# Layer 0 of a four-layer network: products as column tiles, a norm without broadcast rows, whole attention steps, the last gates in two streams on chip

## The chip, the cores and the metric

The kernel runs as one program on one NeuronCore of a Trainium2 chip. Its engines have queues of their own and run side by side: TensorE (PE in the profile, with its weight loads, PEld), VectorE (DVE), ScalarE (ACT), GpSimd (POOL) and SyncE (SP), which here issues most DMAs. The metric is the device time of one execution in microseconds. Before the change three timed runs gave 4085.17, 4080.33 and 4074.14, so a median of 4080.33 us. All data are float32, and a float32 product of this kernel appears in the trace as two records, each of them a weight load and a matmul.

## The reference, cut to layer 0

The network takes x (8 images, 256 channels, 32 x 32) through a convolution and attention layer, a deformable convolution, an attention and feed-forward layer, and an attention and expert layer. The change lies in the first of these:

```python
def _ln(x, w, b):
    r = lax.rsqrt(jnp.mean(x * x, axis=1, keepdims=True) + LN_EPS)
    return x * r * w[:, None, None] + b[:, None, None]

def _attention(x, ...):
    qkv = _bn(_conv1x1(x, qkv_w), ...).reshape(B, NH, 2 * KD + HD, N)
    q, k, v = (qkv[:, :, :KD], qkv[:, :, KD:2 * KD], qkv[:, :, 2 * KD:])
    attn = jax.nn.softmax(jnp.einsum('bhkn,bhkm->bhnm', q, k) * SCALE, axis=-1)
    out = jnp.einsum('bhdm,bhnm->bhdn', v, attn).reshape(B, Cc, H, W)
    pe = _bn(_dwconv3(v_img, pe_w), ...)
    return _bn(_conv1x1(out + pe, proj_w), ...)

def _edffn(x, pi_w, dw_w, fft_p, po_w):
    x = _dwconv3(_conv1x1(x, pi_w), dw_w)
    x1, x2 = (x[:, :hid], x[:, hid:])
    x = _conv1x1(jax.nn.gelu(x1, approximate=False) * x2, po_w)
    ...
    xp = jnp.fft.irfft2(jnp.fft.rfft2(xp) * fft_p, s=(PS, PS))
    ...

def _forward(x, ...):
    x = x + gamma1 * _attention(_ln(x, norm1_w, norm1_b), ...)
    return x + gamma2 * _edffn(_ln(x, norm2_w, norm2_b), ...)
```

Here NH is 4 heads, KD 32, HD 64, N = 1024 positions, the hidden width is 512 (so `pi_w` makes 1024 channels), and the FFT works on patches of 8 x 8.

## The kernel before

`fast0` is layer 0. Channels lie on partitions: an image is a tile of 128 partitions x 2 x 1024 (KC = 2 halves of the channels, N positions, worked on in halves of HF = 512[...]).

**Streams.** Each piece of the work is a Python generator that yields between pieces: `attention()` runs over all batches; `before_attention(b)`, `before_gates(b)`, `gates(b)` and `transforms(b)` each treat one batch. `by_time` merges them: every stream has a start and a step, and the one with the smallest due time is asked for its next piece. Time is counted in yields of the attention, two to a step, so 32 to a batch (T). A compiler pass may move instructions between engines' queues by their dependences afterwards, except those that are pinned[...].

**One attention step** (16 to a batch: two halves of the queries `gq`, eight blocks of keys `kt`) makes the scores `s` of four heads (L1442, four row tiles of 32 x 128 side by side) into two of the PSUM tiles `S`, the exponentials `e` (L1448, ACT), and, after a yield, `values(i - 1)`: the sums of the exponentials on DVE (L1398, L1402) and the products with the values into `A` (L1406, column tiles of 128 x 32). After the eighth block `finish` copies `A` to `av`, sums over keys by a product `D` (L1421), inverts it by Ln and Exp (L1425, L1426), multiplies and adds on DVE (L1428, L1429), makes `proj` (L78) and adds the input (`x`, loaded at L1393, two buffers), and stores to `mid` in DRAM.

**Norm** (`normed`, L1263 to L1285): squares on ACT; the mean over channels as products `ms` in two column tiles of 64, one for each half of the positions (L1272); Ln and Exp to `r`; two products with a row of ones, `rb` (L1281), spread each row over all partitions; ACT copies them from PSUM (L1284); DVE multiplies (L1285).

**Before attention**: norm, `qkv` (L78 through `linear`), the values transposed (`vT`, L1348), and the 3 x 3 depthwise term `pe` by products on three shifted copies (`thrice`, loaded from DRAM at L1361, one buffer).

**Gates**: eight chunks of 128 channels. For each, `pi` (L78) goes through a bank to `hp` (L1487), then a depthwise 3 x 3 convolution to `a`: the middle tap on ACT (L1289), eight taps on DVE (L1296). In the last batch chunks 1 and 7 go through `by_products` instead: 18 products with diagonal matrices `dg` (L1304, L1311). Chunks 0 to 3 pass a gelu (L1512, between two table loads), chunks 4 to 7 multiply them (`gate`, L1501), and the result is stored to `gated` in DRAM (L1502).

**Transforms**: for each of four pairs of patch columns `pr`, `hc` comes back from `gated` (L1526), then `po` (L1540), `fwd` (L1548), a multiply by `gain` (L1550), `back` (L1555), each with an ACT copy out of PSUM, and the residual add (`xc`, L1562) and store (L1563).

All of `qkv`, `proj`, `pi`, `po`, `fwd`, `back`, `ms`, `rb`, `D`, `vT`, `pe` share the two PSUM banks of `bank` (tag X) while attention runs, and four after it. When `attention()` ends, its pools are closed and the rest is merged with `net.head()`, which starts the weights and the first batch of layer 1 (`fast1`). Layer 1's own steps (`row`, `ax`, `ay`, `wt`, and the products `acc`) come after layer 0's last piece in program order, and take space that layer 0 gives up.

`columns` (L1023) and `linear_columns` (L1028) exist already and are used in layer 3; they write one product as four of 32 columns each:

```python
    def columns(self, ps, lhsT, rhs, **flags):
        for h in range(P // 32):
            self.nc.tensor.matmul(ps[32 * h : 32 * h + 32], lhsT=lhsT[:, 32 * h : 32 * h + 32], rhs=rhs, **flags)
```

Of the kernel before, what the change touches and what calls it, by code (L numbers as in the profile page):

```python
# [1156 lines left out]
def fast0(net, io):  # L1157
# [5 lines left out]
    BY_PRODUCTS, HROWS = (1, 7), IMG // 2  # L1163
    yield HOLD
    with ExitStack() as ctx, ExitStack() as att:
# [97 lines left out]
        def normed(xn, x, sq):  # L1263

            squares = [sq(k) for k in range(KC)]
            for k in range(KC):
                nc.scalar.activation(squares[k], x[:, k, :], AF.Square)
            yield
            ps = bank("ms")
            for k in range(KC):  # L1270
                for h in range(2):
                    nc.tensor.matmul(  # L1272
                        ps[64 * h : 64 * h + 64], lhsT=net.mean64, rhs=squares[k][:, bass.ts(h, HF)],
                        start=(k == 0), stop=(k == KC - 1),
                    )
            r = one.tile([P, HF], F32, tag="r", name="r")
            net.rsqrt(r, ps, net.eps6)
            yield
            for h in range(2):
                pr = bank("rb")  # L1280
                nc.tensor.matmul(  # L1281
                    pr, lhsT=net.unit[64 * h : 64 * h + 1, :], rhs=r[64 * h : 64 * h + 1, :], start=True, stop=True
                )
                nc.scalar.copy(squares[0][:, bass.ts(h, HF)], pr)  # L1284
            nc.vector.tensor_tensor(xn, x, squares[0].unsqueeze(1).to_broadcast([P, KC, N]), ALU.mult)  # L1285
# [33 lines left out]
        def before_attention(b):  # L1319
# [6 lines left out]
            def projected(d, w, j, norm):  # L1326
                for h in range(2):
                    ps = bank("qkv")
                    net.linear(ps, w, xn, bass.ts(j, P), bass.ts(h, HF))
                    nc.scalar.activation(d[:, bass.ts(h, HF)], ps, AF.Identity, scale=sc(norm), bias=sh(norm))  # L1330
# [11 lines left out]
            for t4 in range(0, NT, 4):  # L1342
                for t2 in (t4, t4 + 2):
                    ps = bank("vT")
                    for i in range(2):
                        for c in range(KC):
                            lo = i * C + c * P
                            nc.tensor.transpose(ps[:, lo : lo + P], v[:, c, bass.ts(t2 + i, P)], net.ident)  # L1348
                    nc.scalar.copy(va[:, t2 : t2 + 2].rearrange("p t c d -> p (t c d)"), ps)
                yield  # L1350
# [31 lines left out]
        def attention():  # L1382
# [4 lines left out]
            def values(i):  # L1387
                b, gq, kt = steps[i]
                e = es.pop(i)
                first, last = kt == 0, kt == NT - 1  # L1390
                if first:
                    state["x"] = atwo.tile([P, KC, HF], F32, tag="x", name="x")
                    nc.sync.dma_start(out=state["x"], in_=io.src[b][:, :, bass.ts(gq, HF)])  # L1393
                    state["A"] = psA.tile([P, KC, HF], F32, tag="A", name="A")
                elif kt == 1:
                    state["sum"] = aone.tile([P, NH, HF], F32, tag="sum", name="sum")
                    for j in range(2):
                        nc.vector.tensor_tensor(state["sum"][:, 2 * j : 2 * j + 2], state["e"][j], e[j], ALU.add)  # L1398
                else:
                    for j in range(2):  # L1400
                        half = state["sum"][:, 2 * j : 2 * j + 2]
                        nc.vector.tensor_tensor(half, half, e[j], ALU.add)  # L1402
                state["e"] = e
                for c in range(KC):
                    for h in range(NH):
                        nc.tensor.matmul(  # L1406
                            state["A"][32 * h : 32 * h + 32, c, :], lhsT=vas[b][:, kt, c, 32 * h : 32 * h + 32],
                            rhs=e[h // 2][:, h % 2, :], start=first, stop=last,
                        )
                if last:  # L1410
                    later.append(finish(b, gq, state["A"], state["sum"], state["x"]))
                    next(later[0])

            def finish(b, gq, A, total, x):
# [17 lines left out]
                for c in range(KC):  # L1432
                    ps = bank("proj")
                    net.linear(ps, wproj, o, bass.ts(c, P), cols)
                    nc.scalar.activation(av[:, c], ps, AF.Identity, bias=sh(6 + c))
# [3 lines left out]
            for i, (b, gq, kt) in enumerate(steps):  # L1439
# [9 lines left out]
                yield  # L1449
                later = [f for f in later if next(f, f) is None]  # L1450
                if i:
                    values(i - 1)
                yield
            values(len(steps) - 1)
            for f in later:
                for _ in f:
                    yield

# [9 lines left out]
        def before_gates(b):  # L1468
            xn = xs[b] = one.tile([P, KC, N], F32, tag="xn2", name="xn2")
            nc.sync.dma_start(out=xn, in_=mids[b])  # L1470
            yield

            def square(k):
                return five.tile([P, N], F32, tag="a", name="sq") if k else one.tile([P, N], F32, tag="sq", name="sq")

            yield from normed(xn, xn, square)
            yield

        def gates(b):
            xn = xs.pop(b)  # L1480

            def convolved(i):
                hp = two.tile([P, N], F32, tag="hp", name="hp")
                for h in range(2):
                    ps = bank("pi")
                    net.linear(ps, wpi, xn, bass.ts(i, P), bass.ts(h, HF))
                    nc.scalar.activation(hp[:, bass.ts(h, HF)], ps, AF.Identity, bias=pib[:, i : i + 1])  # L1487
                a = cv[i] = five.tile([P, N], F32, tag="a", name="a")
                yield
                if b == B - 1 and i in BY_PRODUCTS:  # L1490
                    yield from by_products(a, hp, i)
                else:
                    yield from depthwise(img(a), img(hp), lambda t_: dw_taps[:, i, t_ : t_ + 1])

            cv, sts = {}, {}

            def gate(j):
# [4 lines left out]
                nc.sync.dma_start(out=gated[b][:, j], in_=sts.pop(j))  # L1502

            for j in (0, 2):
# [3 lines left out]
                for i in (j, j + 1):  # L1508
                    sts[i] = two.tile([P, 4, 2, P], F32, tag="st", name="st")
                    a = cv.pop(i)  # L1510
                    for pc in range(2):
                        net.pinned(nc.scalar.activation(paired(sts[i], pc), patches(a, pc), AF.Gelu))  # L1512
                net.pinned(nc.scalar.preload_act_table_set("natural_log_exp_and_others"))
                yield
                gate(j)
                yield from convolved(5 + j)
# [3 lines left out]
        def transforms(b):  # L1520
# [12 lines left out]
            for pr in range(4):  # L1533
# [4 lines left out]
                for pc in range(2):  # L1538
                    for k in range(4):
                        nc.tensor.matmul(  # L1540
                            ps[:, bass.ts(pc, C)], lhsT=hc[:, k, pc, :], rhs=wpo[:, k, :],
                            start=(k == 0), stop=(k == 3),
                        )
# [3 lines left out]
                ps = bank("fwd")  # L1547
                nc.tensor.matmul(ps, lhsT=fwd, rhs=u.rearrange("p t c -> p (t c)"), start=True, stop=True)  # L1548
                nc.scalar.copy(u.rearrange("p t c -> p (t c)"), ps)  # L1549
                nc.vector.tensor_tensor(u, u, gain.unsqueeze(1).to_broadcast([P, 2, C]), ALU.mult)  # L1550
                yield
                back = bank("back")
                for c in range(KC):
                    for pc in range(2):
                        nc.tensor.matmul(  # L1555
                            back[:, (2 * c + pc) * P : (2 * c + pc + 1) * P], lhsT=u[:, pc, bass.ts(c, P)],
                            rhs=inv, start=True, stop=True,
                        )
                nc.scalar.copy(u.rearrange("p t c -> p (t c)"), back)
                for c in range(KC):  # L1560
                    xt = x[:, c, :].rearrange("p (h q w) -> p q h w", q=2, w=16)
                    nc.vector.tensor_tensor(xt, u[:, c].rearrange("p (q h w) -> p q h w", q=2, w=16), xt, ALU.add)  # L1562
                nc.sync.dma_start(out=io.dst[b][:, :, bass.ts(pr, C)], in_=x)  # L1563
                yield


        T = 32
        main = attention()
        streams = [(0, 1, main)]
        for b in range(B):  # L1570
            streams += [
                (T * (b - 1) - 2, 32 / 21, before_attention(b)) if b > 1 else (11 * b, 1.0, before_attention(b)),
                (T * (b + 1) + 7.4, 0.9, before_gates(b)),
                (T * (b + 1) + 10.5, 32 / 44, gates(b)),
                (T * (b + 2) + 11.5, 2, transforms(b)),
            ]
        for _ in range(10):
# [3 lines left out]
        own["X"], own["diag"] = io.pool(ctx, "f0t", 4, PSUM), io.pool(ctx, "f0d", 2)  # L1581
        by_time(rest + [[T * B + 1, 2, net.head()]])

# [1780 lines left out]
```

## Time and profile before

| | |
|---|---|
| timed runs, median (lowest to highest) | 4080.33 us (4074.14 to 4085.17) |
| the profiled execution: its time, its span | 4139.9 us, 4138.1 us |
| mean granted TensorE clock | 0.949 |
| busy, share of the span: PE, PEld, DVE, ACT, POOL | 91%, 43%, 61%, 55%, 14% |
| layer 0's exponentials L1448 | 256, from 52.5 to 1191.7 us |
| layer 0's last residual add (L1562) | 1407.66 us |
| layer 1's first product into `acc` (L1737) | 1412.05 us |

The profile is that of one execution. A row of the groups names a line, an engine, an operation with its output and inputs, the shape and the number of records, then the busy time in us and the mean length of one in ns, then the idle time of the engine before them and what ended it. Records of matmuls overlap, and their ends are modelled, so the time between two starts tells more than a length. A row of the timeline has the start in us, the time it covers, the engine and line, and in brackets the idle time before it and what ended that. Some matmul records are missing from the trace.

### The profile page before, as it was taken

To read this page: it belongs to the slowest core of one execution; us is meant where nothing else is said; L and a number is where in the kernel's file an instruction comes from. 1 tells how busy PE (TensorE), PEld (TensorE's weight loads), DVE (VectorE), ACT (ScalarE), POOL (GpSimd) and SP (SyncE) were. 2 spreads that over 40 slices of the span, in tenths; PEclk is the share of its full clock that TensorE was granted. 3 is DMA by queue.
4 is the path that set the end of the run, shared out by engine and by line. 5 is a ranking of instruction groups with operands and counts; after the bars stand their busy time and mean duration, and the time that the engine had idled before them with its cause. 6 is when DMAs were issued, how large, how long until landed. Compare 5 with 4: busy or idle time off the path is not lost. (4 is left out here: it accounts for less than half of the span.)

```text
span 4138.1 us, 59047 instructions
## 1 busy us (share of the span) xinstructions
PE 3755.4 (91%) x22502; PEld 1791.9 (43%) x22502; DVE 2522.3 (61%) x5030; ACT 2296.6 (55%) x3122; POOL 571.5 (14%) x646
## 2 busy tenths in 40 slices
PE   8999999999978787889999969899999999998997
PEld 3323333333334444454444525663333333326886
DVE  2398798798896489942232255753365666567345
ACT  4556656556553377734334345535776666675554
POOL 0000000000000000000000012431000150044653
PEclk9999999999888898989999979999999999999998
DMA  3313223223121578720000012432320141055666
GB/s 101 114 44 112 100 69 122 94 72 116 64 98 52 175 257 291 266 84 21 21 21 21 31 51 95 132 122 76 108 97 27 39 141 39 22 160 185 204 214 220
DMA packets 209974, 442.64 MB, mean 107 GB/s; under 512 B 22025, under 2 KB 132572, under 8 KB 197140
## 3 DMA queue, kind: packets, MB, share of 16 engines
q1 hardware_dynamic: 186580, 387.21, 28.4%
q0 software_dynamic: 19440, 46.45, 3.4%
q10 hardware_dynamic: 3664, 5.11, 0.4%
q8 instruction: 181, 2.97, 0.3%
q14 instruction: 109, 0.89, 0.1%
HBM read 283.34 MB, written 162.28 MB: 108 GB/s over the span
## 5 line engine op out<-in xcount | busy, mean ns | idle before, releaser
L1296 DVE SCALAR_TENSOR_TENSOR a<-hp,w_f_vec,a 128x961 f32<-128x961 f32 (+1 forms) x496 | 609.1, 1234 | 105.3 <-ACT a L1289 96.6
L2763 ACT ACTIVATE e<-s,five 128x1024 f32<-128x1024 f32 x512 | 542.8, 1112 | 218.1 <-PE s L2757 207.9
L2757 PE MATMUL s<-q,k 32*128 32x512 f32 x2048 | 312.4, 641 | 0.7 <-issue 0.5
L2737 PE MATMUL A<-e,v 128*32 128x512 f32 x2048 | 275.5, 610 | 17.7 <-DVE o L2742 16.0
L1448 ACT ACTIVATE e<-s 128x1024 f32<-128x1024 f32 x256 | 250.3, 1024 | 71.6 <-PE s L1442 60.9
L1402 DVE TENSOR_TENSOR sum<-sum,e 128x1024 f32<-128x1024 f32 x192 | 230.7, 1221 | 86.5 <-ACT e L1448 86.5
L1406 PE MATMUL A<-e,va 128*32 128x512 f32 x2048 | 265.6, 618 | 0.0
L2445 DVE SCALAR_TENSOR_TENSOR junk<-mo_x,w_f_wr 128x256 f32<-128x256 f32 x512 | 250.0, 488 | 13.5
L78 PE MATMUL pi<-xn,w_l_wpi 128*128 128x512 f32 x512 | 244.4, 619 | 14.2 <-ACT u L1549 9.2
L1442 PE MATMUL s<-q,k 32*128 32x512 f32 x1024 | 180.8, 648 | 2.5 <-ACT e L1448 2.5
L2964 PE MATMUL h<-xk,w 128*128 128x128 f32 x1192 | 155.6, 283 | 22.0 <-DVE xk L2950 14.8
L1058 POOL DMA_INDIRECT res<-y,to x149 | 150.5, 1010 | 134.4 <-DVE y L2988 75.6
L1753 PE MATMUL acc<-wt,z 128*64 128x192 f32 (+4 forms) x1344 | 130.0, 337 | 39.8 <-DVE wt L1808 39.2
L2757 PEld LDWEIGHTS s<-q,k 32*128 32x128 f32 x2048 | 93.3, 183 | 167.8 <-issue 160.9
L2964 PEld LDWEIGHTS h<-xk,w 128*128 128x128 f32 x1192 | 150.9, 198 | 29.2 <-DVE xk L2950 15.8
L78 PEld LDWEIGHTS pi<-xn,w_l_wpi 128*128 128x128 f32 x512 | 95.2, 196 | 152.4 <-issue 114.2
L2933 ACT COPY w<-w_l3f_w 128x512 f32 x149 | 92.1, 629 | 123.5 <-PE h L2964 82.8
L1058 POOL DMA_INDIRECT so<-xl,rows x128 | 130.4, 1019 | 172.1 <-issue 146.9
L1487 ACT ACTIVATE hp<-pi,pib 128x512 f32<-128x512 f32 x128 | 87.3, 691 | 120.2 <-PE pi L78 120.2
L2984 PE MATMUL y<-w_l3f_w,hid 128*128 x596 | 147.1, 389 | 3.8 <-issue 1.6
L1357 POOL MEMSET thrice<- 32x128 f32 x32 | 6.3, 197 | 1012.7 <-PE pe L1373 1012.7
L2258 PE MATMUL y<-w_l2f_w,hid 128*128 128x256 f32 x512 | 126.5, 402 | 17.4 <-issue 17.2
(412 smaller groups left out, 6959.0 us busy)
## 6 DMA issues: line engine op xcount, KB each, us to landing
row<-shifts SPq DMA_DIRECT2D x144, 512.0 KB
x<-d SPq DMA_DIRECT2D x31, 1024.0 KB
xs<-so SPq DMA_DIRECT2D x73, 260.0 KB
so<-zero SPq DMA_DIRECT2D x5, 3380.0 KB
thrice<-vimg SPq DMA_DIRECT2D x64, 256.0 KB
gated<-st SPq DMA_DIRECT2D x32, 512.0 KB
hc<-gated SPq DMA_DIRECT2D x32, 512.0 KB
xl<-mox SPq DMA_DIRECT2D x64, 256.0 KB
```

What stands on the lines that cost most here:

```text
L78: self.nc.tensor.matmul(ps, lhsT=w[:, i, m], rhs=src[:, i, cols], start=(i == 0), stop=(i == k - 1))
L1058: made = self.nc.gpsimd.indirect_dma_start(**args)
L1296: nc.vector.scalar_tensor_tensor(to, fr, taps(t_), to, ALU.mult, ALU.add)
L1402: nc.vector.tensor_tensor(half, half, e[j], ALU.add)
L1406: nc.tensor.matmul(state["A"][32 * h : 32 * h + 32, c, :], lhsT=vas[b][:, kt, c, 32 * h : 32 * h + 32], rhs=e[h // 2][:, h % 2, :], start= ...
L1442: nc.tensor.matmul(ss[h // 2][:, h % 2], lhsT=ks[b][32 * h : 32 * h + 32, bass.ts(kt, P)], rhs=qs[b][32 * h : 32 * h + 32, bass.ts(gq, HF) ...
L1448: nc.scalar.activation(es[i][j], ss[j], AF.Exp, scale=SCALE)
L2445: nc.vector.scalar_tensor_tensor(junk, xn[:, t, :], 1.0, self.wr[:, e, :], ALU.mult, ALU.mult, accum_out=pr[:, t, e : e + 1])
L2737: nc.tensor.matmul(A[32 * h : 32 * h + 32], lhsT=vs[b][:, kt, c * P + 32 * h : c * P + 32 * h + 32], rhs=e[:, h, :], start=first, stop=last,)
L2757: nc.tensor.matmul(ss[h // 2][:, h % 2], lhsT=ks[b][32 * h : 32 * h + 32, c, bass.ts(kt, P)], rhs=qs[b][32 * h : 32 * h + 32, c, bass.ts(h ...
L2763: anchor[:] = [nc.scalar.activation(e[:, 2 * j : 2 * j + 2], ss[j], AF.Square, scale=SCALE, bias=five)]
L2964: nc.tensor.matmul(ps[:, j, m], lhsT=ws[j][:, k, bass.ts(m, P)], rhs=xk[:, j, k], start=(k == 0), stop=(k == KC - 1),)
```

## The change

1. `qkv`, `proj`, `pi`, `po`, `fwd` and `back` are written as four column tiles of 32.
2. The norm makes the mean in four column tiles of 32 for each half of the positions, so that all 128 partitions hold it; Ln takes it from PSUM, one Exp follows; `r`, `rb` and the copies are gone. Both squares of the second norm are taken from the tag `a`, and `xn2` has two buffers.
3. An attention step is one piece instead of two: scores and exponentials, `values(i - 1)`, one piece of each waiting `finish`, yield. T is 16, and the starts and steps of the streams are given anew. `x` has one buffer and is loaded at `kt == 4`.
4. `vT` yields after each bank; `before_gates` has one yield more; `gate(j)` comes after the first piece of the next chunk.
5. The last batch: chunks 1 and 5 go by products; `begun` runs chunks in two streams in turn; the gated tiles stay on chip (`kept`), its transforms are in `gates`, with the first three chunks of `po` for all four `pr` ahead of the last gate, into four banks; `hp` has four buffers there (`late`), `diag` one.

```diff
-            ps = bank("ms")
-            for k in range(KC):
-                for h in range(2):
-                    nc.tensor.matmul(
-                        ps[64 * h : 64 * h + 64], lhsT=net.mean64, rhs=squares[k][:, bass.ts(h, HF)],
-                        start=(k == 0), stop=(k == KC - 1),
-                    )
-            r = one.tile([P, HF], F32, tag="r", name="r")
-            net.rsqrt(r, ps, net.eps6)
-            yield
             for h in range(2):
-                pr = bank("rb")
...
-                nc.scalar.copy(squares[0][:, bass.ts(h, HF)], pr)
+                ps = bank("ms")
+                for k in range(KC):
+                    for j in range(4):
+                        nc.tensor.matmul(
+                            ps[32 * j : 32 * j + 32], lhsT=net.mean64[:, :32], rhs=squares[k][:, bass.ts(h, HF)],
+                            start=(k == 0), stop=(k == KC - 1),
+                        )
+                nc.scalar.activation(squares[0][:, bass.ts(h, HF)], ps, AF.Ln, bias=net.eps6)
+            nc.scalar.activation(squares[0], squares[0], AF.Exp, scale=-0.5)
+            yield
...
-                    net.linear(ps, w, xn, bass.ts(j, P), bass.ts(h, HF))
+                    net.linear_columns(ps, w, xn, bass.ts(j, P), bass.ts(h, HF))
...
-                yield
-                later = [f for f in later if next(f, f) is None]
+                waiting = later[:]
                 if i:
                     values(i - 1)
+                for f in waiting:
+                    if next(f, f) is f:
+                        later.remove(f)
                 yield
...
+            def begun(*chunks):
+                made = [convolved(i) for i in chunks]
+                for m in made:
+                    yield next(m)
+                todo = [(m for n in made[:-1] for m in n), made[-1]]
+                while todo:
+                    for t_ in todo[:]:
+                        if next(t_, "over") == "over":
+                            todo.remove(t_)
+                    yield
...
+            if products:
+                yield from begun(0, 4, products[0])
+                gelus(0, 1)
+                yield from begun(2, 3, products[1])
+                gate(0)
+                gate(1)
...
+                gelus(2, 3)
...
+                yield from made[0]
+                gate(2)
+                yield from made[1]
+                for pr in range(4):
+                    banks[pr] = bank("po")
+                    outward(banks[pr], lambda k: sts[k][:, pr], range(3))
+                    yield
+                gate(3)
+                for pr in range(4):
+                    outward(banks[pr], lambda k: sts[k][:, pr], (3,))
...
+                for pr in range(4):
+                    forward(us[pr])
+                    yield
+                for pr in range(4):
+                    backward(b, pr, us[pr], x[:, :, bass.ts(pr, C)])
+                    yield
...
-                (T * (b - 1) - 2, 32 / 21, before_attention(b)) if b > 1 else (11 * b, 1.0, before_attention(b)),
-                (T * (b + 1) + 7.4, 0.9, before_gates(b)),
-                (T * (b + 1) + 10.5, 32 / 44, gates(b)),
-                (T * (b + 2) + 11.5, 2, transforms(b)),
+                (T * (b - 1) - 1, T / 23, before_attention(b)) if b > 1 else (5.5 * b, 0.46, before_attention(b)),
+                (T * (b + 1) + 3.6, 0.75, before_gates(b)),
+                (T * (b + 1) + 7.6, 0.3 if last else T / 44, gates(b, BY_PRODUCTS if last else ())),
             ]
+            if not last:
+                streams.append((T * (b + 2) + 8, 1, transforms(b)))
```

## The prediction

> **What bounds the kernel now.** I read the page's slices first, then a table of busy time by stretch over the first third of the span (the only part that the change touches), then who waited for whom in it, then the instructions in order of time at the end of layer 0. The attention steps of layer 0 run from 52 to 1200 us, one batch in 142.4 us; its last batch's gates and transforms fill 1200 to 1408; layer 1's first product into `acc` starts at 1412. The chain of waits followed back from the end reaches only some 400 us back, so it does not speak of this part; I take layer 0 to stand wholly on the path, because layer 1's steps begin only when it gives up its space. Of the table (columns: stretch, us, then busy us of PE, PEld, DVE, ACT, POOL, granted clock, DMA share, GB/s):
>
> ```profile
> 762.00:905.00 143.00, 134.96 (x706) 52.79 (x703) 119.74 (x113) 87.07 (x110) 0.79 (x4) 0.99 0.31 101
> 1250.00:1300.00 50.00, 49.22 (x163) 25.02 (x156) 25.73 (x26) 18.95 (x27) 0.00 (x0) 0.98 0.10 33
> 1350.00:1402.00 52.00, 31.02 (x107) 21.48 (x107) 19.54 (x27) 19.63 (x27) 0.00 (x0) 0.84 0.67 233
> ```
>
> A steady batch is TensorE's (135 of 143 us), with VectorE close behind (120). In the tail neither is full: at 1250 PE works and DVE idles, at 1350 both idle. The waits of PE in the steady stage, 192 to 1047 us, six batches (engine and line, waiting for; us in total, times, longest):
>
> ```profile
> PE D L1421 <- ACT v L1284: 11.7, 5, 2.3
> PE pi L78 <- ACT u L1549: 7.7, 5, 1.5
> PE vT L1348 <- ACT sq L1284: 7.0, 6, 1.2
> PE pi L78 <- ACT v L1330: 5.0, 5, 1.1
> ...
> PE ms L1272 <- ACT k L1330: 3.7, 5, 0.8
> ...
> PE rb L1281 <- ACT r L94: 2.3, 6, 0.4
> ```
>
> The rows for D, vT, ms and rb (24.7 us) belong to the norm: L1284 copies its broadcast row out of a bank that the next product wants. The pi rows (12.7) are evictions late behind gelus.
>
> **Column tiles.** Does a product in four column tiles cost more? Starts tell, since ends are modelled:
>
> ```profile
> 604.56 3.60 PE L78 MATMUL pi<-xn,w_l_wpi 128*128 128x512 f32 x8
> 608.09 1.14 PE L1442 MATMUL s<-q,k 32*128 32x512 f32 x8
> ...
> 1199.85 1.92 PE L1406 MATMUL A<-e,va 128*32 128x512 f32 x16
> ...
> 1201.59 1.04 PE L1421 MATMUL D<-sum,unit 128*32 128x512 f32 x8
> ```
>
> Four whole products took 3.53 us to the start of another shape; two products in columns 1.74 us to the start of the same shape, 0.87 each. A record of 512 columns streams 0.43 us, so 3.53 is 8 x 0.43 + 0.09: **0.09 us is the price of changing the array's shape**. [...] The change turns 864 matmuls (pi 256, qkv 128, proj 64, po 256, fwd 32, back 128) into 3456. [...] The row says about nothing: four tiles start some 7 ns apart and run together. By busy time the nearest column group is dearer by little:
>
> ```profile
> L78 PE MATMUL pi<-xn,w_l_wpi 128*128 128x512 f32 x512 | 244.4, 619 | 14.2 <-ACT u L1549 9.2
> ...
> L1026 PE MATMUL qk<-xn,w_l_wq 128*32 128x512 f32 x512 | 62.5, 592 | 1.5 <-issue 1.5
> ```
>
> 244.4/256 is 0.955 us a product, 62.5/64 is 0.977; x 448 products of 512 columns, and half of that for po, is 13 us. Bounds 0 and +13 us; I take 0, because the starts carry no modelled end.
>
> **Shape changes.** In the order in which the two kernels are built, PE changes shape 483 times before and 331 times after while attention runs (65 and 41 in a steady batch): 152 x 0.093 = **-14 us**. Below nothing it cannot cost.
>
> **The norm.** Before: `ms` in two tiles 1.72 us of streaming, `rb` 0.86, Ln 0.69 and Exp 0.63 in between, two copies 0.59 each. After: `ms` in four tiles for each half, 4 x 0.86 = 3.44 us, two Ln, one Exp over 1024. PE: +0.86 x 15 norms = **+13 us**. ACT is level (2.50 against 2.4). The waits of the list go, 24.7 x 7/6 = **-29 us**; what is late next on the same bank ring is the Ln, which runs while the second half streams. The DVE multiply (2.29) stays. Both squares now take `a` buffers: at most three chunks and two squares live, five buffers.
>
> **Whole steps.** Exps of a step no longer stand between halves; all else follows s and A. I walked one built batch (steps 60 to 75) with the rows' durations. Most groups hide: four products in a row need an eviction of 0.69 each 1.72. Two places don't. (1) From the end of fwd, ACT has copy 0.6, gelus with their two table loads 2 x 1.28 + 4 x 0.55 = 4.8, two evictions 1.4, an exp 1.0, a first tap 1.15 and an exp 1.0 = 10.0; PE in that time pi 3.4, s 1.1, A 1.9, back 1.0, 0.3 of changes = 7.7, then s waits 2.3. (2) With vT: PE 1.2 + 1.9 + 0.5 + 1.7 + 1.0 = 6.3 to the second bank of pi; ACT 1.2 + 2.1 + 4.8 + 0.6 = 8.7 to the copy that frees it: 2.4. So 4.7 x 7 = 33 us, in place of the pi waits (12.7 x 7/6 = 15): **+18 us**; bounds 0 (ACT ahead) and +40. D and proj move behind A, later than now, so cheaper or nothing. `x` becomes one buffer: its load waits on SP for the store to `mid`, with `thrice` loads behind it; PE has pe, po, s, A and pi (about 14 us) before it reads them, against an x add, a store and a load (about 12): nothing, at worst 2 us a pass.
> Batch 6's gates start 2.35 steps later (step 119.6 instead of 117.25 of 128). That moves 12 of DVE's taps (84 instead of 72 left after the last sum) and about 9 us of PE's pi, po, fwd and back out of the steady stage: **-9 us** here, paid in the tail.
> Attention stage: -14 + 13 - 29 + 18 - 9 = **-21 us**.
>
> **The tail.** Before, from the last sum at 1200.6 to `acc` at 1412.05, 211 us:
>
> ```profile
> 1258.16 10.13 DVE L1296 SCALAR_TENSOR_TENSOR a<-hp,w_f_vec,a 128x961 f32<-128x961 f32 x8 [8.30 <-ACT a L1289]
> ...
> 1281.51 0.76 DVE L1562 TENSOR_TENSOR xc<-u,xc 128x256 f32<-128x256 f32 x2 [12.09 <-ACT u L1559]
> ...
> 1356.79 1.30 DVE L1501 TENSOR_TENSOR st<-st,a 128x512 f32<-128x512 f32 x2 [12.56 <-ACT a L1317]
> ...
> 1368.14 5.28 PE L1540 MATMUL po<-w_l_wpo,hc 128*128 128x256 f32 x16 [12.01 <-DMA hc<-gated]
> ```
>
> DVE waits for the chunks that PE makes by products (L1311), then the last gates go to DRAM and back (1358 to 1368) and four transforms follow one by one to 1408. After: to the end of the normed xn2 DVE has 31 taps x 1.23 and others, 49 + 2.3 = 51 us (before 49). From there PE's own order is pi 27.5, dw 31, po 27, fwd and back 13, off and z 5, changes 2 = 106 us, and DVE has 94 less layer 1's share; they are now level, so I followed both queues. The one diagonal tile is no bound: its second filling, 9 x 0.33 us on ACT, comes after the first's products, and its reader later still. But chunk 4's first tap stands on ACT behind the first half of `dw` (DVE idle 4), chunk 2's behind gelus (3), chunk 3's behind the second `dw` (5), last gate at +101, then a quarter of po, four copies, fwd, multiply, back, copy and add, +115; z8 and `acc` at +118 to +121. Sum 51 + 120 = 171: **-40 us**. The bounds: -62 (DVE never waits: 51 + 94 + 4) and -10 (half clock, which PE had from 1228 to 1252, holds another 30 us). Layer 1's lead (three `wt` ready at 1384) shrinks to two, but DVE idled then before it could go on, so nothing more.
>
> **Sum.** -21 - 40 = -61 us of the profiled execution, whose own time is 4139.9 (span 4138.1): 4079. The three timed runs have their median at 4080.33, 1.4% lower; in their proportion -60: **4020 us**.
>
> **Rivals.**
> - *The two gelu places cost nothing and the steady batch falls by 6.7 us instead of 2.0* (33 us less): for it, ACT is only 61% busy; against it, its order is fixed and both stand in it. 3987 us.
> - *PE in the tail is the bound at low clock*, and the tail gives 12 instead of 40: for it, clocks of 0.75 to 0.86 in three of the four tail stretches; against it, idle PE came with them. 4048 us.
> - *Slower: evictions behind the exps.* All products share two banks in the steady stage, and whole steps bunch them, so each group's second eviction could stand behind an exp pair of 2.05 us. If 8 of a batch's 11 groups wait so, 16.4 x 7 = 115 us: 4020 + 115 - 19 (places counted already) = 4116 us. It decides from about 5.5 groups a batch (60 + 19 us). Against it: each exp pair comes first and A (1.85) covers it.
> - *The change doesn't do what it says*: the built order has no store to `gated` for the last batch and no `rb`; excluded.
>
> **How the numbers follow.** Forecast 0.50, the free gelus 0.22, the slow tail 0.19, slower 0.09. The forecast's own range by its bounds is 3995 to 4050; with the free gelus and the slow tail beside it, 3982 to 4060 leaves out the slower one and some edges, 0.2. A difference under 0.3% (12 us) cannot be told from none; of the slow tail 0.05 falls there. Faster 0.86, same 0.05, slower 0.09.
>
> **What would show it.** Changes of shape at 0.09 us with a column product at 0.87 us; no PE wait on a norm copy; a PE wait behind gelus of about 2.4 us twice a batch; a steady batch of about 140.4 us (-2.2 changes, +1.7 norm, -4.1 norm waits, +2.6 gelus); DVE's tail without an idle of 12 us, and `acc` about 171 us after the last sum. A steady batch above 143, or `acc` later than 200, would prove me wrong.

## Result, and the profile after

The changed kernel's median is 4027.14 us (4018.52 to 4030.78, 4 runs), that of the kernel before in the same set of runs 4078.43 (4074.14 to 4085.17, 4 runs). The ratio is **0.987**, 95% interval 0.9848 to 0.9891: 51 us faster.

The two profiled executions differ by more, 4139.9 against 4028.2 us. Reading both at the first `acc`, where layer 0's tail ends, sorts this out: 1412.0 us from the span's start before, 1354.6 after, 57.4 us earlier. The other 54 us lie behind `acc`, where almost nothing was changed. In all fourteen profiles of this study the stretch from `acc` to the end took either 2672 to 2677 us or 2724 to 2747 us, whatever the kernel. In the twelve experiments it goes with the chip that they ran on (the timed runs as well: the kernel before has medians of 4083 us on one chip and of 4136 to 4155 on two others), so the kernel before was most likely profiled on a chip of the longer sort, the changed one on the other. The time up to `acc` does not depend on that: two executions of the same program on two chips (the changed kernel and e4) had `acc` at 1354.6 and 1353.6 us. So below, **the time of the first `acc` is what I compare**, with the timed ratio beside it. It is read from one execution each, so how well it repeats rests on this one pair. The expectations count 11.2 us more for it, because they start at the trace's first record and not at the span's.

Busy time by stretch, changed kernel (start:end, length, then busy us and instructions of PE, PEld, DVE, ACT, POOL; granted clock, DMA share, GB/s). The first row is a steady batch, the others the tail:

```profile
741.00:894.00 153.00, 144.22 (x1444) 48.14 (x1440) 128.62 (x119) 93.09 (x117) 0.78 (x4) 0.98 0.31 97
1228.00:1278.00 50.00, 47.67 (x368) 17.09 (x372) 35.95 (x37) 21.60 (x37) 0.00 (x0) 0.95 0.18 58
1278.00:1328.00 50.00, 44.70 (x460) 20.88 (x454) 40.21 (x40) 17.56 (x25) 0.00 (x0) 0.93 0.12 38
1328.00:1355.00 27.00, 24.61 (x418) 14.07 (x412) 19.13 (x30) 16.91 (x25) 0.50 (x2) 1.00 0.70 226
```

In the tail PE is now near full where it used to stand at 31 of 52 us. The steady batch has not become shorter: between the starts of its exps batches 4 to 6 took 153.6 us each before and 154.9 after. All of the attention stage's gain (last sum from 1199.4 to 1178.1, 21.3 us) was made in batches 0 to 2 (19.3 us) and in the last one.

Waits of PE in the same 192 to 1047 us as before:

```profile
PE pe L1367 <- DMA thrice<-vimg: 21.7, 6, 4.4
PE s L1437 <- ACT e L1443: 9.5, 11, 3.4
PE po L1026 <- DMA hc<-gated: 8.7, 4, 2.4
PE pi L1026 <- ACT va L1343: 8.3, 4, 2.1
PE qkv L1026 <- DVE xn L1280: 7.6, 5, 3.3
```

The waits for norm copies are gone from the list; the `thrice` wait on top of it was not among the waits of the kernel before. The product groups of layer 0, busy us and mean ns of a record:

```profile
L1026 PE MATMUL pi<-xn,w_l_wpi 128*32 128x512 f32 x2048 | 245.2, 618 | 15.9 <-ACT va L1343 8.3 <-DVE gn_t L1717 5.5 <-ACT u L1476 2.1
...
L1026 PE MATMUL qkv<-xn,w_f_wqk 128*32 128x512 f32 x512 | 57.4, 593 | 0.0
```

Four times the records of `pi` fill the same 245 us (244.4 before): the four column tiles of a product run side by side. DVE's idles in the tail, with what ended each in brackets:

```profile
1253.28 10.13 DVE L1291 SCALAR_TENSOR_TENSOR a<-hp,w_f_vec,a 128x961 f32<-128x961 f32 x8 [5.71 <-ACT a L1284]
...
1276.57 10.13 DVE L1291 SCALAR_TENSOR_TENSOR a<-hp,w_f_vec,a 128x961 f32<-128x961 f32 x8 [4.46 <-ACT a L1284]
1291.25 5.05 DVE L1291 SCALAR_TENSOR_TENSOR a<-hp,w_f_vec,a 128x961 f32<-128x961 f32 x4 [4.55 <-ACT a L1284]
1308.02 8.88 DVE L1291 SCALAR_TENSOR_TENSOR a<-hp,w_f_vec,a 128x961 f32<-128x961 f32 x7 [4.53 <-ACT a L1284]
```

No idle of 8 or 12 us is left, but four of 4.5 to 5.7, each a first tap on ACT that stands behind something.

### The profile page after: what moved, and what is told of

Same layout as the page of the kernel before. It is cut to its first block, busy times and chain, and to the rows that moved or that the text cites. A ratio compares the mean times of both kernels' runs of the same rounds, so it can differ in the third digit from the quotient of the medians.

```text
span 4026.3 us, 70004 instructions
## 1 busy us (share of the span) xinstructions
PE 3691.7 (92%) x28006; PEld 1696.4 (42%) x28006; DVE 2527.2 (63%) x5030; ACT 2296.6 (57%) x3106; POOL 569.6 (14%) x646
## 5 line engine op out<-in xcount | busy, mean ns | idle before, releaser
L1291 DVE SCALAR_TENSOR_TENSOR a<-hp,w_f_vec,a 128x961 f32<-128x961 f32 x496 | 610.7, 1233 | 94.2 <-ACT a L1284 84.8
L1026 PE MATMUL pi<-xn,w_l_wpi 128*32 128x512 f32 x2048 | 245.2, 618 | 15.9 <-ACT va L1343 8.3
L1401 PE MATMUL A<-e,va 128*32 128x512 f32 x2048 | 248.5, 603 | 0.1
L1819 PEld LDWEIGHTS acc<-wt,z 128*64 128x64 f32 x1344 | 99.3, 152 | 101.6 <-DVE wt L1874 72.2
L1026 PEld LDWEIGHTS pi<-xn,w_l_wpi 128*32 128x32 f32 x2048 | 67.9, 113 | 161.9 <-issue 135.2
```

Of the source, the lines that this page charges most:

```text
L1291: nc.vector.scalar_tensor_tensor(to, fr, taps(t_), to, ALU.mult, ALU.add)
L1401: nc.tensor.matmul(state["A"][32 * h : 32 * h + 32, c, :], lhsT=vas[b][:, kt, c, 32 * h : 32 * h + 32], rhs=e[h // 2][:, h % 2, :], start= ...
L1819: nc.tensor.matmul(acc[o, a * IMG : e * IMG], lhsT=zs[b][:, c, t, :], rhs=wt[:, c, (a - lo) * IMG : (e - lo) * IMG], start=False, stop=(t ...
```

## Experiments

| kernel | ratio to before, 95% | last sum | sum to `acc` | first `acc`, us | steady batch |
|---|---|---|---|---|---|
| before | 1 | 1199.4 | 212.7 | 1412.0 | 153.6 |
| changed | 0.987 (0.9848-0.9891) | 1178.1 | 176.5 | 1354.6 | 154.9 |
| e4, same program | 0.9852 (0.9827-0.9877) | 1177.0 | 176.6 | 1353.6 | 155.1 |
| e1 old tail | 0.998 (0.9966-0.9995) | 1176.5 | 220.1 | 1396.7 | 154.6 |
| e2 full products | 0.9847 (0.9822-0.9872) | 1172.9 | 170.9 | 1343.8 | 153.8 |
| e3 old norm | 0.9914 (0.9892-0.9937) | 1197.1 | 177.9 | 1375.0 | 158.8 |
| e5 thrice on POOL | 0.9883 (0.9857-0.991) | 1179.8 | 176.5 | 1356.3 | 156.8 |
| e6 old steps | 0.9787 (0.9765-0.9809) | 1148.7 | 174.3 | 1323.0 | 147.1 |
| e7 before + tiles | 1.0008 (0.9995-1.0021) | 1193.3 | 209.0 | 1402.3 | 154.0 |
| e8 e2 + e5 | 0.9924 (0.99-0.9948) | 1193.5 | 173.3 | 1366.8 | 158.2 |
| e9 new steps, old starts | 0.9891 (0.9866-0.9915) | 1189.5 | 170.2 | 1359.6 | 153.8 |
| e10 old steps, three new starts | 0.9877 (0.9857-0.9898) | 1176.8 | 173.0 | 1349.8 | 153.5 |
| e11 e6 + full products | 0.9787 (0.9764-0.9811) | 1154.4 | 164.6 | 1319.0 | 147.6 |
| e12 e6, squares later | 0.981 (0.9793-0.9827) | 1153.0 | 170.0 | 1323.0 | 147.9 |

("Steady batch" is the mean of batches 4 to 6, counted from 0; the other times are read from one execution each. Each ratio is to the kernel before on the same chip. The ratios bear out the large steps: against e4, e1 loses about 53 us by them, e3 26, and e6 gains 27. They do not resolve 10 us.)

**e1, the old tail.**

```diff
-                if i in products:
+                if b == B - 1 and i in BY_PRODUCTS:
-(T * (b + 1) + 7.6, 0.3 if last else T / 44, gates(b, BY_PRODUCTS if last else ())),
+(T * (b + 1) + 7.6, T / 44, gates(b)),
-            if not last:
-                streams.append((T * (b + 2) + 8, 1, transforms(b)))
+            streams.append((T * (b + 2) + 8, 1, transforms(b)))
```

(with chunks 1 and 7 and two diagonal tiles again)

> The changed kernel, but batch 7's gates go through DRAM as in the other batches, in chunk order, with chunks 1 and 7 by products and a transforms stream at the end. Theory (the tail gave 36 to 40 us, none of it given back): 4063 to 4067 us, 0.996 to 0.997 of before, the tail from the last sum to acc back from 176 to some 212 us, with the 12 us DVE wait for the gelus and the 12 us wait for hc there again. Rival (the tail is shorter only because the rest of the kernel reaches it in a better clock window, the new order itself is worth a third): 4039 us. Rival of the predicted 'slow tail': less than 12 us lost.

`acc` came 43 us later than in e4, the last sum at the same time. Both waits are back, 10.5 us each (DVE's is for a chunk by products, L1312, as in the kernel before, and not for gelus, as the expectation has it):

```profile
1343.65 1.29 DVE L1533 TENSOR_TENSOR st<-st,a 128x512 f32<-128x512 f32 x2 [10.54 <-ACT a L1312]
```

```profile
1353.46 5.60 PE L1026 MATMUL po<-w_l_wpo,hc 128*32 128x256 f32 x64 [10.46 <-DMA hc<-gated]
```

(the first from DVE's, the second from PE's order of time in e1). The theory holds; the slow-tail rival is out.

**e2, e7 and e11, column tiles against full products.** e2 takes the tiles out of the changed kernel, e7 puts them alone into the kernel before, e11 takes them out of e6.

```diff
-net.linear_columns(ps, wpi, xn, bass.ts(i, P), bass.ts(h, HF))
+net.linear(ps, wpi, xn, bass.ts(i, P), bass.ts(h, HF))
```

(and so for qkv, proj, po, fwd and back)

> The changed kernel with qkv, proj, pi, po, fwd and back again as full 128-column products; the norm keeps its four column tiles. Theory (each change of the PE array's tile shape costs 0.09 us, some 150 more of them; the tiled product itself costs nothing extra): 14 us slower, 4041 us. [...] If neither matters because PE waits elsewhere anyway: within 4 us of 4027.

> The kernel before with the column tiles in qkv, proj, pi, po, fwd and back, and nothing else of the change. Prediction's step (135 fewer changes of tile shape at 0.093 us, the tiles free): 12 to 13 us faster than before, first acc 1410 us. As in e2, where full products were 10 us faster up to acc in spite of 80 more shape changes: 10 us slower, first acc 1433 us. [...]

> e6 with full products in place of the column tiles, the norm apart. By shape changes (159 more, at 0.093 us): 15 us slower than e6, first acc 1349 us, ratio 0.982. As in e2 (full products 10 us earlier at acc, with fewer and shorter PE waits): first acc 1324 us, ratio 0.976.

Up to `acc`, with about 80 more shape changes, e2 is 9.8 us *faster* than e4, which the timed ratio does not show. With 135 fewer, e7 is 9.7 us faster than before (12.6 at the price of 0.093), but its timed ratio shows nothing. With 159 more, e11 is 4.0 us faster than e6 up to `acc` and the same by the ratio. With 2592 matmuls fewer (e2, e11) or more (e7), none of the three moved by more than 10 us up to `acc`. In e2 PE is busier from 192 to 1047 us (809.0 us against the changed kernel's 796.9), as the price of the changes has it, but it waits less: 13.9 us for `thrice` against 21.7. The two stages differ in sign, too: up to the last sum the tiles are worth 6.1 us in e7 and 5.7 between e11 and e6, and they cost 4.1 in e2; behind it the full products are 5.7 us faster in e2 and 9.7 in e11, but 3.7 slower in e7, which has the old tail. So the sign seems to depend on which waits the shifted order meets, and up to `acc` the tiles are worth no more than 10 us either way.

**e3, the old norm.**

```diff
-            for h in range(2):
-                ps = bank("ms")
...
-            nc.scalar.activation(squares[0], squares[0], AF.Exp, scale=-0.5)
+            r = one.tile([P, HF], F32, tag="r", name="r")
+            net.rsqrt(r, ps, net.eps6)
+            for h in range(2):
...
+                nc.scalar.copy(squares[0][:, bass.ts(h, HF)], pr)
```

> The changed kernel with the old norm (64-column means, the factor r, two broadcast products and two copies). Theory (the waits for the copies were on PE's path, 29 us over 16 norms, less 13 us of PE that the new norm costs): 16 us slower, 4043 us, with PE waits of rb or ms on ACT in the trace. Rival (the waits had gone by the scheduler's new order alone, so the old norm is the cheaper one): 13 us faster, 4014 us.

21 us later at `acc`, 20 of it before the last sum. The steady batches take 158.8 us. The size is the theory's, a little larger, and the rival is out. The theory's way is not shown: of the waits for the norm's copies (L1284), 18.7 us in the kernel before, little came back from 192 to 1047 us, and no wait of `rb`:

```profile
PE vT L1347 <- ACT sq L1284: 4.0, 6, 0.7
```

`D` has no wait for a copy there. Up to the last sum PE is idle 84.0 us, against 74.6 in e4, its `s` is cut 37 times instead of 32 (below), and it has some 47 more changes of shape; how these make up the 20 us is open.

**e4, e5 and e8, the wait for `thrice`.** SP's queue in the changed kernel, then PE's row that it ends in:

```profile
851.73 0.57 SPq L1432 DMA_DIRECT2D mid<-x  x1
...
856.03 0.40 SPq L1397 DMA_DIRECT2D x<-in_x_dram  x1
...
857.40 1.42 SPq L1355 DMA_DIRECT2D thrice<-vimg  x3
```

```profile
864.97 4.20 PE L1367 MATMUL pe<-thrice,w_f_wpe 128*32 128x512 f32 x24 [3.93 <-DMA thrice<-vimg]
```

The load of `x`, with one buffer, follows the store to `mid` by 4.3 us, and `thrice` is issued 1.4 us behind it.

```diff
-                if kt == 4:
+                if kt == 6:
                     state["x"] = aone.tile(...)
```

> The changed kernel with x loaded at key tile 6 instead of 4, when the store of mid that reads the same buffer has long landed. Theory (SP stands at x's load until mid has landed, the loads of thrice queue behind it, and PE waits 3.6 us a batch for them): PE's wait for thrice falls from 21.7 us to under 3, the kernel is 15 to 25 us faster, 4002 to 4012 us. Rival A (thrice waits behind mid's own store, which waits for DVE's sum): the wait falls by less than half, 4020 us. Rival B (PE's wait only moves on to the next thing that is late, the exps): the thrice wait is gone and the time is 4025 to 4029 us.

This edit moved nothing: the load is placed where its buffer comes free, whatever key tile it is written at, and every engine's order is that of the changed kernel. It serves as a second measurement of the changed kernel, and its theory stays untested. e5 takes `thrice` off the queue instead, e8 does so with e2's full products:

```diff
-                        nc.sync.dma_start(
+                        nc.gpsimd.dma_start(
                             out=thrice[32 * j : 32 * j + 32, :, lo - n : hi - n],
```

> The changed kernel with the loads of thrice issued by POOL instead of SP. (The run before this one, e4, turned out to be the same program as the changed kernel on every engine: the load of x goes to where its buffer comes free, whatever key tile it is written at. So that theory is still untested, and e4 stands as the changed kernel on this chip: 0.985 of before, first acc 1365 us.) Theory (SP's queue holds the loads back): PE's wait for thrice falls from 22 us in seven batches to under 6, first acc 10 to 20 us earlier, ratio 0.981 to 0.983. Rival A (the transfers themselves are late, because mid, x, xc and hc land in the same stretch): the wait stays above 15 us, within 4 us. Rival B (the wait goes, and the next late thing, the exps and the xn of qkv, takes its place): wait under 6 us, first acc less than 5 us earlier.

> The changed kernel with both full products (as e2) and thrice on POOL's queue (as e5). If the two are independent, their gains add: e2's first acc of 1355 us less what e5 shows, and a ratio of 0.980 to 0.983. If both remove the same wait (e2's gain came with thrice waits of 15 instead of 22 us): no better than the better of the two.

PE's waits in e5, 192 to 1047 us:

```profile
PE po L1026 <- DMA hc<-gated: 20.8, 4, 5.8
...
PE pe L1367 <- DMA thrice<-vimg: 6.7, 5, 2.5
```

SP's queue did hold `thrice` back: its wait fell from 21.7 to 6.7 us. But `hc`, which used to be issued ahead of one of these groups of loads (822.8 against 824.2 us), is now issued behind it (817.9 against 817.1), and `po` waits 12 us longer. That the two loads share the DMA engines, whose busy share is 0.92 from 817 to 825 us in e5, is the likely reason; no run separates them. `acc` is 2.7 us later than in e4: rival B in its effect (though the wait is 6.7 us, where it had under 6), with another successor than the one I named. e8 comes out 13 us later than e4 and 23 later than e2, with 17.1 us of `hc` waits: the two edits don't add.

**e6, e9, e10 and e12, steps and starts.** e6 gives the attention loop its half steps back, and all streams their old starts and paces, except the last gates' pace:

```diff
-                waiting = later[:]
-                if i:
-                    values(i - 1)
-                for f in waiting:
...
+                yield
+                later = [f for f in later if next(f, f) is None]
+                if i:
+                    values(i - 1)
                 yield
...
-        T = 2 * NT
+        T = 32
-(T * (b + 1) + 7.6, 0.3 if last else T / 44, gates(b, BY_PRODUCTS if last else ()))
+(T * (b + 1) + 10.5, 0.6 if last else 32 / 44, gates(b, BY_PRODUCTS if last else ()))
```

> The changed kernel with the old half steps in the attention loop and the old start and pace of all streams except the last gates' pace; x keeps one buffer, the norm, the column tiles and the end stay new. Prediction's step (the gelus' new places cost 2.3 and 2.4 us a batch, less 9 us for batch 6's gates): this kernel is 9 to 18 us faster than the changed one, first acc 1347 to 1356 us. Rival (what is left of the attention stage's 21 us after 19 for the norm and minus 5 for the column tiles is the new order's): 7 us slower, first acc 1372 us.

`acc` comes **30.6 us earlier** than in e4: the prediction's step had the sign and too small a size. One cost of a whole step can be read in PE's order of time. In the changed kernel:

```profile
876.29 1.14 PE L1437 MATMUL s<-q,k 32*128 32x512 f32 x8
...
880.68 1.13 PE L1437 MATMUL s<-q,k 32*128 32x512 f32 x4 [0.41 <-ACT e L1443]
882.63 1.13 PE L1437 MATMUL s<-q,k 32*128 32x512 f32 x4 [0.82 <-ACT e L1443]
```

The four heads' `s` of a step are row tiles that run side by side: 8 records take 1.14 us. When an exp is late, the second pair waits for its bank (or another product is put between), and 4 records take as long as 8. A late exp so costs its wait (here 0.82 us) and about 1 us more, and PE's list of waits does not show the second. Call it a cut where two of a step's eight records of `s` start more than 0.65 us apart. A steady batch has three cuts or more in the changed kernel, in three of its 16 steps; two in the kernel before, both in one step; none in e6.

Is it the whole steps, or the starts? e9 keeps the steps and takes the old starts (first diff, against the changed kernel), e10 the old steps with the new starts of `before_gates`, `gates` and `transforms` (second, against e6). Not shown in the diffs: in e9 the other old starts and the old yields of `vT` and `before_gates`, in e10 the extra yield of `before_gates`.

```diff
-(T * (b + 1) + 3.6, 0.75, before_gates(b)),
-(T * (b + 1) + 7.6, 0.3 if last else T / 44, ...
+(T * (b + 1) + 3.7, 0.45, before_gates(b)),
+(T * (b + 1) + 5.25, 0.3 if last else T / 44, ...
```

```diff
-(T * (b + 1) + 7.4, 0.9, before_gates(b)),
-(T * (b + 1) + 10.5, 0.6 if last else 32 / 44, ...
-(T * (b + 2) + 11.5, 2, transforms(b))
+(T * (b + 1) + 7.2, 1.5, before_gates(b)),
+(T * (b + 1) + 15.2, 0.6 if last else 32 / 44, ...
+(T * (b + 2) + 16, 2, transforms(b))
```

> The other half of e6 (which had first acc at 1334 us, 31 us before the changed kernel): the new whole steps in the attention loop stay, but every stream but the last gates' pace has its old start and pace, in whole steps (gates from 5.25 instead of 7.6, before_gates from 3.7 at 0.45 without its extra step, transforms from 5.75, two pairs of va to a step). Theory A (the whole steps put the exps, gelus and copies in the worse order, whatever the starts): first acc within 8 us of the changed kernel's 1365. Theory B (the later start of gates and the spread of its streams does it): first acc 1334 to 1342 us, and steady batches of 147 us. In both, the number of PE waits of 2 us and more times some 5 us (the wait and half of the 3.4 us window at half clock that follows each) should account for the difference of the batches.

> e6 with the new kernel's starts for three streams, in half steps: before_gates from 7.2 at 1.5 with its extra step between xn2's load and the squares, gates from 15.2, transforms from 16; the attention loop and before_attention stay old. Theory (PE's longest wait in e6, 3.0 us a batch of ms for the squares of xn2, goes with the extra step, and with it the half clock window of 3.4 us that follows it): steady batches of 142 to 143 us, first acc 1305 to 1315 us. Rival (the late gates start is what costs e6's gain, theory B of e9): steady batches of 150 to 154 us, first acc 1355 to 1370 us.

Both have steady batches of 153 to 154 us. e9 came out as its theory A (`acc` 6 us later than e4), e10 as its rival (4 us earlier, where its theory had 50 or more). Only the old steps with the old starts reach 147: each half of the move alone loses nearly all of it, and neither theory A nor B is the whole. Nor do long waits alone account for e9: it has one in most batches (4.0 to 5.6 us against 3.0 in e6), yet its batch is 6.7 us longer; it has four cuts of `s` a batch.

In e6 the longest wait left stands behind the landing of xn2, and PE waits with ACT (order of time of both engines):

```profile
767.62 2.00 ACT L1267 ACTIVATE sq<-xn 128x1024 f32<-128x1024 f32 x2 [4.37 <-DMA xn<-mid]
...
768.73 2.79 PE L1273 MATMUL ms<-sq,mean 128*32 128x512 f32 x12 [2.89 <-ACT sq L1267]
```

e12 puts one more half step between them:

```diff
+            yield
             yield from normed(xn, xn, square)
-(T * (b + 1) + 10.5, 0.6 if last else 32 / 44, ...
+(T * (b + 1) + 11.4, 0.6 if last else 32 / 44, ...
```

> e6 with one more half step between xn2's load and its squares, and the streams behind it moved by the same 0.9 (gates from 11.4, transforms from 12.4). In e6 ACT stands 4.4 us a batch at the squares for the landing of xn2, PE waits 2.9 us behind it, and a window at half clock follows each time. Theory (that wait was e6's last long one, and only the squares need the step): no PE wait of 2 us in the steady batches, 143 to 144 us a batch, first acc 1312 to 1318 us, ratio 0.974. Rival (as in e9 and e10, each shift of a stream lays a new conflict elsewhere): a wait of 2 us or more at another product, batches of 147 us or more, first acc 1334 us or later.

In batches 4 to 6 no wait of PE is over 1.4 us and the clock stays full, as the theory said, but the batches take 147.9 us and `acc` is at the same 1323.0: the rival in time, without a long wait in its place. `s` is now cut four times a batch, and not by waits of its own. Of these two rows of PE neither has a wait; `pi` and `qkv` stand between them:

```profile
756.08 1.13 PE L1438 MATMUL s<-q,k 32*128 32x512 f32 x4
...
765.40 1.13 PE L1438 MATMUL s<-q,k 32*128 32x512 f32 x4
```

A count from the traces, from 45 us to the last sum, tells what the lists of waits leave out. "Lost to the clock" is the time times what the granted clock lacks of 1, an upper bound, since it counts idle time too:

| kernel | stage, us | PE idle (gaps over 0.15 us) | lost to the clock | shape changes | cuts of `s` |
|---|---|---|---|---|---|
| changed | 1133.1 | 74.9 | 39.3 | 333 | 33 |
| e6 | 1103.7 | 70.0 | 18.8 | 287 | 12 |
| e9 | 1144.5 | 68.1 | 29.0 | 345 | 41 |
| e10 | 1131.8 | 80.9 | 32.4 | 314 | 18 |
| e12 | 1108.0 | 54.1 | 13.7 | 353 | 33 |

Against e6, e9's idle, clock and shape changes (at 0.09 us) explain about 13 of its 41 us, and in e12 they would make it 15 us shorter where it is 4 longer; 29 and 21 more cuts at about 1 us fill both gaps. In the changed kernel and in e10 idle, clock and changes alone could make up nearly all of the 29 and 28 us, so there the share of the cuts is open.

So e6 and e11, at 0.979 of the kernel before, beat both kernels: e6 is this change's norm, tiles and tail with the old steps and starts, e11 the same without the tiles.

## Why the prediction was right

The forecast of 4020 us stands 7 us from 4027.14, and its parts' sum of 61 us 4 from the 57.4 measured up to `acc`. Some of its steps were right, others erred against each other, so that the number is in part luck. The sign that was to prove it wrong, a steady batch above 143 us, came: 154.9.

- **The tail** (-40): -36 by the two profiles, 43 when undone in e1. The mis-sized term is DVE's waits for first taps: 4 + 3 + 5 = 12 us predicted, 5.7 + 3 x 4.5 = 19 measured.
- **The norm** (-29 + 13 = -16): nearly right in size, 21 us in e3. The copies' waits went, as predicted; that they are what the old norm costs is not shown, since in e3 hardly any came back.
- **Shape changes and tiles** (-14 and 0): a tiled product costs nothing extra that the trace shows (all `pi` 245.2 us against 244.4) and e7's 9.7 us over 135 changes give 0.07 us for one, near the 0.09. Up to the last sum e7 and e11 give about 6 us, half of the 14; but inside the changed kernel the tiles cost 10 us up to `acc` (e2). I counted a saving on PE as a saving of time; that a shorter PE only meets its late partners earlier is how I read e2's waits, not shown by itself.
- **Whole steps** (+18 for two places behind gelus, -9 for batch 6): the step that failed. Place (2) was right: PE waits 2.1 us for the `va` copy, 2.4 predicted, though in four of the six batches only. Place (1) was there as waits of 0.4 and 0.8 us and one cut of `s` of about 1.1, together the 2.3 predicted, by another way. What failed is the step that most groups hide and two places don't: outside these two, the new order made PE wait 21.7 us for `thrice`, cut `s` at two more steps a batch, and goes with more half clock (39.3 us lost at most, 18.8 in e6). Undone, whole steps and starts are worth 31 us and not 9.
- **"Nothing, at worst 2 us a pass" for `x` with one buffer** was wrong in this order: PE waits 3.1 to 4.4 us a batch for `thrice`. But e6 keeps the one buffer, and there PE's longest idle before `pe`, from 250 to 1047 us, is 0.5 us; so the buffer alone does not make the wait. Taking the loads off SP's queue gained nothing (e5): `po` waited longer instead.
- **The steady batch** of 140.4 us was worked from a wrong base. The 142.4 us that I called one batch is the mean over eight; the first two take 101 and 132 us and a steady one 153.6. It was to fall by 2.0 and rose by 1.3, while batches 0 to 2 fell by 19.3 together.
- **The attention stage** (-21, measured -21.3) is right by luck, as a sum of two errors: without the new steps and starts the rest of the change brings the last sum 50.7 us earlier (e6), where I had -30, and they take back 29, where I had 9. Norm (20 us, e3) and tiles (6 us, e7) tested alone make up only about half of those 51; how the rest arises from both together was not taken apart further.
- **The scale.** I put the 61 us in proportion to the median, as if the profiled execution were slower throughout. Its excess lay behind `acc` only; the difference of 1 us in the forecast was luck.

Of the rivals, the slow tail fell with e1. "Evictions behind the exps" did not come: no eviction wait is in PE's first five rows but the 2.1 us of `va`. "Free gelus" was wrong too. That e6 comes near its 33 us (31 at `acc`, 6.5 in a steady batch) does not confirm it, since e6 has the old steps.

## What to carry to other kernels

Where two orders differ only in where work is placed, count for each product not only what it waits for but also what stops running beside it: a concurrent set of row tiles that an order splits costs its whole duration again (here four records of `s` took 1.13 us, as eight took 1.14), and no list of waits shows it. A saving on the bounding engine is worth its size only as long as its partners (evictions, exps, transfers) are not what it then meets; test each part by undoing it, and compare at a marker right behind the changed stage. An edit of when a load is written is no edit until the built order shows that it moved.

## What the runs showed of the hardware

**A short idle of PE costs more than itself.** Stretches of 3.41 us, or of a multiple of it, at a granted clock of 0.5 lie all over the attention stage (15 in the changed kernel from 190 to 1140 us). Around the `thrice` wait of 861.0 to 865.0 us (granted clock is the third number from the end):

```profile
857.50:861.00 3.50, 3.50 (x54) 1.52 (x46) 3.50 (x4) 0.59 (x1) 0.00 (x0) 1.00 0.77 282
864.50:867.90 3.40, 2.93 (x16) 0.90 (x20) 1.83 (x2) 0.00 (x0) 0.00 (x0) 0.51 0.20 64
868.00:871.40 3.40, 3.40 (x26) 0.84 (x22) 0.09 (x1) 1.80 (x2) 0.19 (x1) 1.00 0.02 5
```

In the second stretch the matmuls of `pe` start 0.82 to 0.85 us apart in sets of four, those of `A` after it, at full clock, 0.43. Over all fourteen profiles, between 190 and 1140 us, 161 of 162 half-clock stretches began in, or within 4 us after, a PE idle of at least 0.7 us: 92 of the 111 idles of 2.5 us and more met one in that time, 42 of the 74 of 1.9 to 2.5 us, and 28 of the 223 shorter ones. A wait of 3 us so costs up to 4.7 (with half of one 3.4 us stretch at half clock, an estimate). That it is not all of the story is seen in e12, whose batches 4 to 6 have no such window (granted clock 1.00 from 717 to 867 us) and take 147.9 us, against 147.1 in e6.

**The time behind `acc` comes in two sizes by chip**, about 2675 and about 2735 us, while the time up to `acc` of the one program that was profiled on two chips repeats to 1 us. Within the longer sort the profiles spread by 23 us, so gains of 10 us up to `acc` drown in the whole time.
